# Layers 0 and 1 of a four-layer graph network: one sum of adjacency quarters by a raw load and an accumulating DMA in place of VectorE, and a list of nodes by the eight largest keys

## The chip, the core and the metric

The kernel runs on one core of one Trainium2 chip. The core has five engines with instruction streams of their own: TensorE (PE, with its weight load PEld), VectorE (DVE), ScalarE (ACT), GpSimd (POOL) and SyncE (SP); 16 DMA engines move data between HBM and SBUF. Plain loads and stores are here issued by SP, a few by ACT; POOL issues stores, indirect transfers and the DMAs that add to their destination. The metric is the device time of one execution in microseconds (us).

## The reference, cut to what matters

Sixteen graphs (batches) of 1024 nodes with 256 features go through four layers, each a pre-normed residual layer on the same adjacency matrix:

```python
h = jnp.maximum(_layernorm(x, axis=-1), 0.0)
x = x + _L0_gnn_ref(h, adj, ...)   # attention: a = adj*exp(e_i+f_j), rows scaled to sum 1; a @ (h W^T + b)
h = jnp.maximum(_layernorm(x, axis=-1), 0.0)
x = x + _L1_gnn_ref(h, adj, ...)   # d^-1/2 adj d^-1/2 @ (h W) + bias
h = jnp.maximum(_layernorm(x, axis=-1), 0.0)
x = x + _L2_gnn_ref(h, adj, ...)   # a recurrence over the nodes, one after the other
h = jnp.maximum(_layernorm(x, axis=-1), 0.0)
x = x + _L3_gnn_ref(h, adj, ...)   # adj @ h, a two-layer MLP with an RMS norm and silu
```

Layers 0 and 1 need, for every batch, the product of the 1024x1024 adjacency with a 1024x256 matrix twice (once per layer), and sums of its rows. Layer 2 walks through the nodes in order; the kernel groups nodes of each block of 128 that do not depend on each other, so it needs, beforehand, an order of the nodes computed from `adj`.

## The kernel before, in words

**Seven products instead of eight.** Each 1024x1024 product is cut into 2x2 blocks and done by Strassen's method in Winograd's form. The adjacency's four blocks of 512x512, each a tile of 128x4x512 fp32 (1 MB), are `b11`, `b21`, `b22` and one that is only used inside `t3`; four sums of blocks are `t1`, `t2 = t1 + b22`, `t3`, and `t4 = t2 + b21`. All live in ten buffers `at0` to `at9`, which the list `quarters` hands out and takes back in turn. `get` loads a block by SP. `plus(b, name, other)` adds one tile to another in place by a DMA that POOL issues (`accum_op=ADD`); it makes `t1` and `t3` of every batch but the first. `add_halves` makes a sum by two VectorE additions of 128x1024 each; it makes `t2` and `t4`. `keep` stores the four sums to HBM for layer 3. `drop` returns a buffer after the last product that reads it.

**`layers_0_1`** writes the order of all five engines out by hand (a manual schedule): instructions run on each engine in the order in which the code records them. A loop over i from 0 to 15 holds, for batch i, the sums of layer 0 (hooks `a0` to `a6`), the weights of layer 0, two pieces of the weights of layer 1 for batch i-1, the sums of layer 1 (hooks `d0` to `d6`), and the row sums (`degrees`) of batch i+1. `sums` (L387) does seven products of eight fp32 matmul passes each, in the order b11, b21, t2, t1, t3, t4 ("22"), b22, and calls one hook after each: so VectorE's and ScalarE's work for the loads, norms and sums of the next batch is laid between the products. VectorE combines the products' results in L397, L407, L411 and L414, and adds the weights' result to x in L427. `weights` (L423) multiplies by the 256x256 weight.

**Names that the change and the steps touch.** `a1` computes two combinations of h (`second`) and then `t4`. `get(i+1, "b11")` and the others fetch the next batch. In the last part of iteration i, `plus(i+1, "t3", "b22")`, the two `keep`s of `t1` and `t2`, one `plus_row` (POOL adds a bias row to a part of x, L362) and the taking of a buffer for `t4` follow each other. Further `plus_row`s stand in `a2_`, `a3`, `a4`. `Moments.first` and `Moments.second` let ScalarE sum and square x of the next batch for its norm (L337, L345); `normed` (L358) scales and cuts h. `inv_sqrt` computes roots on POOL (L86: `rs`, `dis`).

**Jobs.** From i = 9 to 15 two jobs per iteration, `run_a` and `run_b`, prepare layer 2 for two batches: they load `ad`, `ab`, `h2`; `mask` and `scale` (POOL, L524 to L532) change `ad`; `turn` and `order` transpose on PE and copy out by ScalarE and VectorE (L545, L572, L574); POOL stores `heT_d`, `near_d`, `next_d` and `base_d`. All need the node order.

**The order of the nodes.** `orders` is a generator of VectorE work on 128 rows (8 blocks of 16 batches), 128 nodes each. `places` gives each node a bin and a position (`pos`); `rest` then makes the list `node` (which node sits at position p), the index tables, and a chain over the nodes (L205, L206), fetching tiles `pc` by ACT's queue (L105) on the way. Each `yield` states a cost. `side(us)` in the hooks runs the generator until 1.25 times the given budget is used up: this is how the list's work is spread over the loop.

Of the kernel before, what the change touches and what calls it, by code (L numbers as in the profile page):

```python
# [11 lines left out]
ALU = mybir.AluOpType  # L12
# [4 lines left out]
P = 128  # L17
# [19 lines left out]
def bcast_row(ap, n):  # L37

    return bass.AP(tensor=ap.tensor, offset=ap.offset, ap=[[0, P], [1, n]])
# [3 lines left out]
def gnn_stack(ctx: ExitStack, tc: tile.TileContext, a: dict, out: bass.AP):  # L43
    nc = tc.nc
# [23 lines left out]
    step = const.tile([P, P], F32, name="step")  # L68
# [27 lines left out]
    def orders(pool, psum):  # L96
# [5 lines left out]
        def fetch(j0):  # L102
            def run():
                nz = pool.tile([P, R, P], F32, name="pc", bufs=3)
                nc.scalar.dma_start(nz, a["own"][:, j0 : j0 + R])  # L105
                pieces.append(nz)
            later.append(run)

        def piece(j0, op, value):
            nz = pieces.popleft()  # L110
            nc.vector.tensor_scalar(nz[:, :, j0:], nz[:, :, j0:], 0.0, value, op0=op, op1=ALU.mult)
            return nz

        def tile_(name, n=P):
            return pool.tile([P, n], F32, name="o_" + name)

        TOP = 1000.0
        bins, pos = tile_("bins"), tile_("pos")
        junk = tile_("junk")
        open_, below, held, fit = tile_("open", S), tile_("below", S), tile_("held", S), tile_("fit", S)  # L120

        def places():
            nc.vector.memset(bins, TOP)
            nc.vector.tensor_scalar(open_, step[:, :S], -1.0, TOP - 1, op0=ALU.mult, op1=ALU.add)
            nc.vector.tensor_scalar(below, open_, 1.0, None, op0=ALU.add)
            for k in range(S):
                nc.vector.memset(held[:, k : k + 1], -float(ALL_SLICES[k]) if k < NSL else 0.0)
            nc.vector.scalar_tensor_tensor(open_, held, 0.0, open_, op0=ALU.is_lt, op1=ALU.mult)
            for j0 in range(0, 3 * R, R):
                fetch(j0)  # L130
            yield 9.0
            for j0 in range(0, P, R):
                nz = piece(j0, ALU.is_equal, 2 * TOP)
                for j in range(j0, j0 + R):
                    mine = bins[:, j : j + 1]
                    nc.vector.scalar_tensor_tensor(fit, below, mine, open_, op0=ALU.is_le, op1=ALU.mult)
                    nc.vector.tensor_reduce(mine, fit, AX.X, ALU.max)
                    nc.vector.scalar_tensor_tensor(held, open_, mine, held, op0=ALU.is_equal, op1=ALU.add)
                    nc.vector.scalar_tensor_tensor(open_, held, 0.0, open_, op0=ALU.is_lt, op1=ALU.mult)
                    if j + 1 < P:  # L140
                        nc.vector.scalar_tensor_tensor(bins[:, j + 1 :], nz[:, j - j0, j + 1 :], mine, bins[:, j + 1 :],
                                                       op0=ALU.add, op1=ALU.min)
                    if j < j0 + R - 1:
                        yield 1.0
                if j0 + 3 * R < P:
                    fetch(j0 + 3 * R)
                yield 1.2

            key = tile_("key")
            nc.vector.scalar_tensor_tensor(key, bins, -256.0, step, op0=ALU.mult, op1=ALU.add)  # L150
            for i in range(0, P, R):
                less = pool.tile([P, R, P], F32, name="pc", bufs=3)
                nc.vector.tensor_tensor(less, key[:, None].to_broadcast([P, R, P]),
                                        key[:, i : i + R][:, :, None].to_broadcast([P, R, P]), ALU.is_lt)
                nc.vector.tensor_reduce(pos[:, i : i + R], less, AX.X, ALU.add)
                yield 1.4
            pt = psum.tile([P, 512], F32, name="pt")
            nc.tensor.transpose(pt[:, :P], pos, ident)
            nc.vector.tensor_copy(place, pt[:, :P])
            yield 0.5  # L160

        def rest():

            node = tile_("key")
            for p in range(P):
                nc.vector.scalar_tensor_tensor(junk, pos, float(p), step, op0=ALU.is_equal, op1=ALU.mult,
                                               accum_out=node[:, p : p + 1])
                if p % 4 == 3:
                    yield 1.6
            first = tile_("first", 2)  # L170
            nc.gpsimd.iota(first[:, :1], pattern=[[0, 1]], base=0, channel_multiplier=P, allow_small_or_imprecise_dtypes=True)
            of8 = tile_("of8", GB)
# [2 lines left out]
                                           accum_out=first[:, 1:])  # L175
# [25 lines left out]
            for j0 in range(0, P, R):  # L201
                nz = piece(j0, ALU.not_equal, 2.0)
                for j in range(j0, min(j0 + R, P - 1)):
# [3 lines left out]
                                                   op0=ALU.mult, op1=ALU.max)  # L207
# [56 lines left out]
    def layers_0_1():  # L264
        with ExitStack() as st:
# [7 lines left out]
            x, q, h1, h2, g, dis, mean, rs_of, ags = {}, {}, {}, {}, {}, {}, {}, {}, {}  # L273
# [14 lines left out]
            quarters = [big.tile([P, 4, 512], F32, name=f"at{k}") for k in range(10)]  # L288
            Q = {b: {} for b in range(B)}

            def get(b, name, m, n):
                Q[b][name] = quarters.pop(0)
                nc.sync.dma_start(Q[b][name], a["quarters"][b, m, n])

            def drop(b, name):
                quarters.append(Q[b][name])

            def keep(b, name):
                nc.sync.dma_start(t_d[name][b], Q[b][name])

            def plus(b, name, other):
                nc.gpsimd.dma_start(out=Q[b][name], in_=Q[b][other], accum_op=ALU.add)
# [53 lines left out]
            def normed(h, x, shift, scale, tiles):  # L356
                for t in tiles:
                    nc.scalar.activation(h[:, t], x[:, t], AF.Relu, bias=shift[:, t : t + 1], scale=scale[:, t : t + 1])  # L358
# [237 lines left out]
            def side(us):  # L596
                while later:
                    later.popleft()()
                left[0] += us * 1.25
                while left[0] > 0:  # L600
                    cost = next(math, None)
                    if cost is None:
                        break
                    left[0] -= cost
                left[0] = min(left[0], 0.0)

            all_ = range(NT)
            lo, hi = range(NT // 2), range(NT // 2, NT)
# [16 lines left out]
            def add_halves(b, to, left, right):  # L625
                for k in range(2):
                    nc.vector.tensor_add(half(Q[b][to], k), half(Q[b][left], k), half(Q[b][right], k))
# [5 lines left out]
            left_of, first, second = combos(q[0])  # L633
            first()
            add_halves(0, "t3", "t3", "b22")
            Q[0]["t4"] = quarters.pop(0)
            nc.sync.dma_start(vec["bias"], bcast_row(a["bias"], D))
            nc.sync.dma_start(w1, a["weight"].rearrange("(c p) e -> p c e", p=P))
            load_x(1)
# [6 lines left out]
            for i in range(B):  # L646
                run_a, run_b = jobs.get(i, (None, None))
                here, ahead, behind = i < B, i + 1 < B, i > 0
# [8 lines left out]
                def a1():  # L657
                    if ahead:
                        get(i + 1, "b11", 0, 0)
                    second()  # L660
                    add_halves(i, "t4", "t2", "b21")
                def a2_():
                    if ahead:
                        get(i + 1, "t1", 0, 1)
# [24 lines left out]
                def a5():  # L689
                    inverse(i, got["deg"])  # L690
                    if run_a:
                        run_a.scale()
                    if ahead:
                        mean[i + 1].first(hi)
                    side(1.8)
                def a6():
                    if ahead:
                        mean[i + 1].middle()
                        mean[i + 1].second(lo)
                    side(2.0)  # L700
                if here:
                    ag = sums(i, left_of, [a0, a1, a2_, a3, a4, a5, a6])
                    h1[i] = big.tile([P, NT, D], F32, name="h1")
                    m1 = Moments(x[i], "n", h1[i][:, 0])
                    weights(x[i], ag, w0, got["rc"], m1)
                    m1.root()
                    if ahead:
                        mean[i + 1].second(hi)

                def second_weights(pairs):  # L710
# [7 lines left out]
                if here:  # L718
                    rd = small.tile([P, NT], F32, name="rd")
                    nc.vector.tensor_mul(rd, m1.rs, dis[i])  # L720
                    shift = small.tile([P, NT], F32, name="shift")
                    nc.vector.tensor_mul(shift, m1.neg, rd)
                    normed(h1[i], x[i], shift, rd, all_)
                    if ahead:
                        mean[i + 1].root()
                second_weights(pairs)
# [64 lines left out]
                if ahead:  # L791
                    ds = degrees(i + 1)
                    plus(i + 1, "t3", "b22")
                    keep(i + 1, "t1")
                    keep(i + 1, "t2")
                    plus_row(x[i + 1], "W_b", 0)
                    Q[i + 1]["t4"] = quarters.pop(0)
                def late_norm():
                    h2[i - 1] = big.tile([P, NT, D], F32, name="h2", bufs=2)
                    normed(h2[i - 1], x[i - 1], m2.shift, m2.rs, all_)  # L800
# [1007 lines left out]
```

## Time and profile before

Three runs took 4202.88 us in the median (4201.75 to 4206.0). The profiled execution took 4201.68 us; its span, from the first to the last instruction, is 4199.8 us.

| | |
|---|---|
| PE busy | 4008.7 us, 95% of the span |
| PEld busy | 2796.3 us, 67% |
| DVE busy | 2614.5 us, 62% |
| ACT busy | 1634.5 us, 39% |
| POOL busy | 1648.1 us, 39% |
| mean granted TensorE clock | 0.986 |
| layers 0 and 1 (0 to 1330 us): PE, DVE, ACT, POOL busy | 1238.3, 966.2, 705.8, 449.3 us |
| the same: mean DMA share, rate | 0.73, 245 GB/s |
| `add_halves` (L627), 128x1024 | 68 instructions, median 1220 ns |
| list of nodes (L166), 128x128 | 128 instructions, median 291 ns, and 128 reads of the accumulator, 81 ns |
| accumulating DMA `at<-at` (L302) | 30 issues of 1 MB by POOL, 912 ns each in the median, 7.0 us to landing |

A profile row names the line, the engine, the operation and the tiles written and read; "idle before" is the time that the engine stood still ahead of it, with what ended the wait. The granted clock is the share of TensorE's full speed that the throttle allowed. A query of windows gives busy time and DMA share of any stretch; the timeline gives single instructions in order of time. In this profile the first product of batch i starts at 22 us for i = 0, 376 for 5, 445 for 6, 650 for 9, 740 for 10, 833 for 11, 925 for 12, 1021 for 13, 1113 for 14 and 1212 for 15.

### The profile page before, as it was taken

The numbers are of one execution on the slowest core, as the hardware profiler recorded it, in microseconds if no ns is written. First come the engines' busy times: TensorE is split into PE (matmuls) and PEld (weight loads), VectorE is DVE, ScalarE is ACT, GpSimd is POOL, SyncE is SP. The second block draws the span as 40 slices with busy tenths as digits, with TensorE's granted clock in tenths as the row PEclk, the third lists the DMA queues.
The fourth block names the chain that finished last, engine by engine and source line by source line (L and its number), as shares of the span: only waits on it lengthen the run. The fifth ranks groups of instructions, "written<-read, shape, count | busy, mean of one in ns | idle before, by whom it ended". The sixth has DMA issues, their size and how long they took to land. (4 is left out here: it accounts for less than half of the span.)

```text
span 4199.8 us, 56656 instructions
## 1 busy us (share of the span) xinstructions
PE 4008.7 (95%) x19307; PEld 2796.3 (67%) x19307; DVE 2614.5 (62%) x6218; ACT 1634.5 (39%) x4172; POOL 1648.1 (39%) x1740
## 2 busy tenths in 40 slices
PE   7999999999997999999999999998899999999998
PEld 3545455555554888888888888877465665656656
DVE  7888976477762434444444444454677877777776
ACT  3565655545543332322322232333333344333332
POOL 2232223434334324243333333332555364463552
PEclk9999999999999999999999999998999999999999
DMA  7576757988768454646454545431634434334320
GB/s 243 207 237 230 227 201 261 264 297 292 281 211 266 134 185 156 192 132 201 136 187 154 192 144 184 141 124 40 234 113 141 151 121 159 123 130 171 111 100 21
DMA packets 406702, 744.72 MB, mean 177 GB/s; under 512 B 75168, under 2 KB 325664, under 8 KB 365344
## 3 DMA queue, kind: packets, MB, share of 16 engines
q1 hardware_dynamic: 370976, 613.49, 42.6%
q0 software_dynamic: 26080, 109.21, 9.2%
q10 hardware_dynamic: 9216, 16.78, 1.1%
q8 instruction: 209, 3.42, 0.3%
q14 instruction: 221, 1.81, 0.1%
HBM read 538.85 MB, written 183.76 MB: 172 GB/s over the span
## 5 line engine op out<-in xcount | busy, mean ns | idle before, releaser
L86 POOL TENSOR_TENSOR rs<-rs_v,mhalf 128x8 f32<-128x8 f32 (+1 forms) x65 | 112.4, 1729 | 892.4 <-DVE rs_v L82 461.4
L935 PE MATMUL pf<-hb,ab 128*128 128x256 f32 x1568 | 415.2, 383 | 0.0
L1049 PE MATMUL pf<-hs,wx 128*128 128x256 f32 x1536 | 347.8, 382 | 14.5 <-POOL hs L1039 14.2
L1049 PEld LDWEIGHTS pf<-hs,wx 128*128 128x128 f32 x1536 | 291.7, 192 | 56.7 <-POOL hs L1039 15.3
L1592 POOL TENSOR_TENSOR ss<-ss,sq 128x512 f32<-128x512 f32 x224 | 299.6, 1353 | 22.9 <-ACT sq L1590 16.7
L1362 POOL DMA_INDIRECT hs_d<-h,table x128 | 129.3, 1010 | 444.4 <-ACT gates L1057 366.4
L935 PEld LDWEIGHTS pf<-hb,ab 128*128 128x128 f32 x1568 | 272.1, 191 | 37.3 <-issue 6.7
L1054 DVE TENSOR_TENSOR gates<-pf,bias 128x512 f32<-128x512 f32 x128 | 88.5, 692 | 283.5 <-PE pf L1049 249.2
L423 PE MATMUL pmm<-w,ag 128*128 128x256 f32 x1024 | 236.6, 390 | 17.0 <-DVE ag L414 7.6
L1655 PEld LDWEIGHTS po<-w,hh 128*128 128x128 f32 x2048 | 238.3, 193 | 16.6 <-issue 11.0
L1655 PE MATMUL po<-w,hh 128*128 128x128 f32 x2048 | 242.5, 277 | 1.4 <-ACT hh L1638 0.7
L423 PEld LDWEIGHTS pmm<-w,ag 128*128 128x128 f32 x1024 | 198.1, 195 | 57.8 <-DVE x L427 9.9
L1590 ACT ACTIVATE sq<-hh 128x512 f32<-128x512 f32 x224 | 141.6, 632 | 199.7 <-POOL ss L1592 123.0
L1538 PE MATMUL ph<-bxt,hb 128*128 128x512 f32 x440 | 200.7, 602 | 13.1 <-ACT hb L1510 10.5
L1147 ACT ACTIVATE r<-pr 128x128 f32<-128x128 f32 (+2 forms) x256 | 57.9, 278 | 353.4 <-PE pr L1103 293.5
L1085 PE MATMUL pf<-bd,h 128*128 128x384 f32 (+4 forms) x512 | 182.9, 449 | 1.4 <-DVE bxt L1088 1.4
L1088 DVE TENSOR_TENSOR bxt<-bxt,pf 128x384 f32<-128x384 f32 (+4 forms) x256 | 127.7, 501 | 82.1 <-PE pf L1085 79.7
L1588 DVE SCALAR_TENSOR_TENSOR hh<-ph,b,u 128x512 f32<-128x512 f32 x192 | 141.1, 749 | 43.9 <-PE ph L1584 34.1
L1638 ACT ACTIVATE hh<-hh,rw 128x512 f32<-128x512 f32 x256 | 158.9, 711 | 23.8 <-DVE hh L1637 23.8
L1538 PEld LDWEIGHTS ph<-bxt,hb 128*128 128x128 f32 x440 | 82.9, 193 | 111.3 <-issue 92.8
L345 ACT ACTIVATE pt<-x,m_neg 128x256 f32<-128x256 f32 x240 | 114.5, 477 | 107.7 <-DVE m_neg L340 101.3
L1637 DVE TENSOR_TENSOR hh<-hh,po 128x512 f32<-128x512 f32 x256 | 154.3, 679 | 2.9 <-PE po L1634 2.9
(371 smaller groups left out, 9246.8 us busy)
## 6 DMA issues: line engine op xcount, KB each, us to landing
at<-in_quarters SPq DMA_DIRECT2D x94, 1024.0 KB
t_d<-at SPq DMA_DIRECT2D x64, 1024.0 KB
ab<-in_columns SPq DMA_DIRECT2D x127, 512.0 KB
bxt<-t_d SPq DMA_DIRECT2D x42, 1024.0 KB
bxt<-in_quarters SPq DMA_DIRECT2D x34, 1024.0 KB
at<-at POOLq DMA_DIRECT2D x30, 1024.0 KB, 7.0
at<-t_d SPq DMA_DIRECT2D x22, 1024.0 KB
pc<-in_own ACTq DMA_DIRECT2D x64, 256.0 KB
```

Of the source, the lines that this page charges most:

```text
L423: nc.tensor.matmul(po[:, t - t0], ag[:, c, t * P : (t + 1) * P], w[:, c], start=c == 0, stop=c == DC - 1)
L935: nc.tensor.matmul(pb, ab[:, jts[k]], hb[:, jts[k]], start=k == 0, stop=k == len(jts) - 1)
L1049: nc.tensor.matmul(pg[:, e], wx[:, c, q * D + e * P : q * D + (e + 1) * P], self.hs[:, c], start=c == 0, stop=c == DC - 1)
L1085: nc.tensor.matmul(pf, h[:, g, c * P : (c + 1) * P], bd[:, g, b0 : b0 + n, S : S + far], start=True, stop=True)
L1362: nc.gpsimd.indirect_dma_start(out=hs_d[t][g][:, :], out_offset=row(1, g, t, s), in_=h[:, g], in_offset=None)
L1538: nc.tensor.matmul(pa, st[left][:, k], at[q % 6][:, k], start=onto is None and k == 0, stop=k == 3, skip_group_check=True)
L1588: behind3[:] = [nc.vector.scalar_tensor_tensor(hh[q][:, k], ph, b1[:, k : k + 1], u, op0=ALU.add, op1=ALU.add)]
L1590: nc.scalar.activation(sq, hh[q][:, k], AF.Square)
L1592: nc.gpsimd.tensor_tensor(ss[q], ss[q], sq, ALU.add)
L1637: nc.vector.tensor_mul(hh[q][:, k], hh[q][:, k], pr)
L1638: nc.scalar.activation(hh[q][:, k], hh[q][:, k], AF.Silu, scale=rw[:, k : k + 1])
L1655: nc.tensor.matmul(po[:, n], left[:, c, n * P : (n + 1) * P], right[:, c], start=onto is None and n == 0 and c == 0, stop=c == HH - 1, ski ...
```

## The change

1. `t4` is no longer added up by VectorE. A new function `raw_t4` takes the buffer and loads block (1, 0), which is what `b21` holds, into it a second time by SP; in `a1`, `plus(i, "t4", "t2")` adds `t2` to it by an accumulating DMA that POOL issues. The loads stand where the buffer was taken before: behind the `keep`s of `t1` and `t2`.
2. The list of nodes is no longer found position by position. The keys (bin and node in one number) are turned around so that the first node has the largest key; 16 times, `max` takes the eight largest of each row and `match_replace` sets them to 0. Five elementwise instructions and the one that turns the keys give the node's number from the key. The yields of this part sum to 12.8 units instead of 51.2.
3. In iterations with jobs, the budgets of `side` in `a5` and `a6` fall from 1.8 and 2.0 to 0.8 and 0.0.
4. In iterations with jobs, `mean[i + 1].second(hi)` (ScalarE) moves from behind the weights of layer 0 to behind `normed`, which stands after `run_a.turn`.

```diff
             nc.vector.scalar_tensor_tensor(key, bins, -256.0, step, op0=ALU.mult, op1=ALU.add)
+            nc.vector.tensor_scalar(bins, key, -1.0, 127.0, op0=ALU.mult, op1=ALU.add)
...
-            for p in range(P):
-                nc.vector.scalar_tensor_tensor(junk, pos, float(p), step, op0=ALU.is_equal, op1=ALU.mult,
-                                               accum_out=node[:, p : p + 1])
-                if p % 4 == 3:
-                    yield 1.6
+            for p in range(0, P, 8):
+                nc.vector.max(out=node[:, p : p + 8], in_=bins)
+                nc.vector.match_replace(out=bins, in_to_replace=node[:, p : p + 8], in_values=bins, imm_value=0.0)
+                yield 0.8
+            whole = 1.5 * 2.0 ** 31
+            nc.vector.tensor_scalar(junk, node, whole, None, op0=ALU.add)
+            nc.vector.tensor_scalar(junk, junk, whole, None, op0=ALU.subtract)
+            nc.vector.tensor_sub(node, junk, node)
+            nc.vector.tensor_scalar(node, node, 127.0, None, op0=ALU.add)
...
+            def raw_t4(b):
+                Q[b]["t4"] = quarters.pop(0)
+                nc.sync.dma_start(Q[b]["t4"], a["quarters"][b, 1, 0])
...
-            Q[0]["t4"] = quarters.pop(0)
+            raw_t4(0)
...
                     second()
-                    add_halves(i, "t4", "t2", "b21")
+                    plus(i, "t4", "t2")
...
-                    side(1.8)
+                    side(0.8 if run_a else 1.8)
...
-                    side(2.0)
+                    side(0.0 if run_a else 2.0)
...
-                    if ahead:
+                    if ahead and not run_a:
                         mean[i + 1].second(hi)
...
                     normed(h1[i], x[i], shift, rd, all_)
+                    if ahead and run_a:
+                        mean[i + 1].second(hi)
                     if ahead:
                         mean[i + 1].root()
...
-                    Q[i + 1]["t4"] = quarters.pop(0)
+                    raw_t4(i + 1)
```

## The prediction

> **What bounds the kernel now.** The page's busy table says TensorE (PE) 95%, VectorE (DVE) 62% of a 4199.8 us span. Its chain of waits covers only the last third, so it says nothing of layers 0 and 1, where every edit lies. I therefore read the table of windows (layers 0 and 1 end near 1330 us; PE is busy 1238.3 of those 1330 us), then the waits of PE there, in the two halves of the loop over batches. Columns: waiting op, what released it, total us, times, longest. First i = 1 to 8 (60 to 680 us), then i = 9 to 14 (680 to 1210 us), where the jobs `run_a` and `run_b` are added:
>
> ```profile
> PE pmm L423 <- DVE x L427: 4.5, 4, 1.4
> PE pz L387 <- DVE ag L407: 3.2, 6, 0.8
> ```
>
> ```profile
> PE pt L542 <- ACT pt L345: 8.1, 6, 2.2
> PE pmm L423 <- DVE ag L414: 7.6, 4, 3.5
> PE pt L565 <- ACT hT L572: 7.4, 6, 3.2
> ...
> PE pmm L423 <- DVE ag L411: 2.8, 1, 2.8
> PE pz L387 <- DVE ag L407: 2.1, 3, 1.1
> PE pmm L423 <- DVE x L427: 1.9, 1, 1.9
> ```
>
> PE is the bound, and DVE costs time only where PE waits for it: 7.7 us in the first half, 14.4 us in the second. A wait has a second price. Around the 3.48 us wait at 1050.5 us of i = 13, the windows read (PE, PEld, DVE, ACT, POOL busy, then clock, DMA share, GB/s):
>
> ```profile
> 1047.00:1054.00 7.00, 3.52 (x18) 2.75 (x16) 6.72 (x17) 0.00 (x0) 4.09 (x4) 1.00 1.02 427
> 1054.00:1058.00 4.00, 4.00 (x11) 2.84 (x12) 3.75 (x19) 3.16 (x11) 0.00 (x0) 0.58 0.82 315
> ```
>
> After the gap the granted clock is 0.58: the next 32 weight matmuls (L423) take 8.96 us, against 7.07 us for 32 undisturbed ones at 1285.7. The same comparison gives 1.8 us in i = 11, 3.7 us in i = 12 (14.2 us for 48 against 10.5), 1.8 us in i = 14: 9.2 us with i = 13's 1.9.
>
> **The change, part by part.**
>
> *Sum t4 leaves VectorE.* Out: 2 adds of 128x1024 per batch, 32 in all; a pair takes 2.35 us where nothing disturbs it (387.5 us), so 37.6 us. They stood in `a1`, ahead of every DVE step of the first sums that PE then waits for (L407, L411, L414, L427).
>
> *Node list.* Out: 128 instructions that follow each other every 0.335 us (600 us), 43 us. In: 16 `max` and 16 `match_replace`, in no row of the trace; nearest are a 128x128 scalar_tensor_tensor (0.29 us) and a reduction of 128x128 (0.38 us). A pair costs 0.5 us if each is like these, 1.0 us if `match_replace` counts double; I take 0.65, so 10 us, plus 6 elementwise 128x128 steps at 0.28. Net 31 us of DVE out, in i = 7 to 9; PE waits for DVE there 0.99 us (680 us), so this alone is worth next to nothing, at either price. Its yields fall from 51.2 to 12.8 units, so what follows (tables, then the chain, L205) comes one batch earlier: chain in i = 10 to 14 instead of 11 to 15. The 2.9 us wait of L225 for L226 at 1210 us moves to i = 14, behind the product of t2, and I let it cost the same.
>
> *Budgets.* In i = 9 to 14 `a5` gives 0.8 instead of 1.8 and `a6` 0 instead of 2.0; times 1.25 that is 3.75 us less list work ahead of L414 and L427. With the adds, DVE arrives some 6 us earlier than now at the step for which PE waits 2.8 to 3.5 us. But POOL's scaling of `ad` (L531, L532, 3.6 us at 1047.6) runs beside two-input DVE steps that stretch under it (L490: 1.60 us, alone 0.17), so a rest stays.
>
> *second(hi) after normed.* 4 squares and 4 accumulator reads, 2.6 us of ScalarE, stood ahead of the four copies of `turn` (L545), for which PE waited 8.1 us in six batches. Behind `normed` ScalarE next waits 2.4 us for PE anyway (1073.8), and POOL, whose `rs` comes 3 us later, next waits 5.4 us for DVE (1077.6). Gain 7.5; late next are the copies themselves, 0.2 us each.
>
> *What t4 adds.* 16 loads of 1 MB on SP's queue, issued behind `keep` of t2, and 16 accumulating DMAs on POOL's queue. POOL now waits for load and t2; behind it stand three `plus_row` (3.9 us of POOL) and `dis`; behind those nothing is due before the weights. SP's `keep` of t4 waits for the landing. The load takes 1 MB / 430 GB/s = 2.4 us, the accumulation 7.0 us (median of `at<-at` to landing). PE needs t4 at the product "22". For i = 6, PE's rows:
>
> ```profile
> 444.52 3.70 PE L387 MATMUL px<-at,q 128*128 128x512 f32 x8
> ...
> 463.50 3.68 PE L387 MATMUL py<-at,q 128*128 128x512 f32 x8
> ```
>
> SP issues `keep` of t2 at 441.5, so the load lands near 449; POOL is free at 446. The accumulation of t3 has the queue until about 453 (451 now), then 7 us: 460, 3.5 us ahead of 463.5. In i = 13 POOL's near_d, next_d and base_d precede it (last issue 1023.4) and its queue drains by 1028; 7 us more: 1035, with PE at 1039.7. So no wait, but little to spare.
>
> Here **a rule speaks against the change**. The Trainium skill, "DMA: Bandwidth & Descriptors", section Queues, rings and completion order: each DMA engine takes turns between its queues, packet by packet. SP's loads are queued at the same moment, so an even share would make the 7 us 14: landing at 1042 in i = 13 (2.3 late) and 467 in i = 6 (3.5 late), over 6 and 9 batches some 45 us. The trace answers with the queue's share at 1026 to 1028 us, when SP had issued two loads of 1 MB:
>
> ```profile
> q0 software_dynamic: 152, 0.51, 95.2%
> q1 hardware_dynamic: 1, 0.00, 0.1%
> ```
>
> POOL's queue (q0) had nearly all of the engines and SP's (q1) nothing. I take the row; the rule makes the rival below. The price falls on SP's loads: 9.4 us later per batch. The engines idle 434 to 442 and 470 to 484 in i = 6's neighbourhood, 962 to 974 and 1058 to 1068 later on, so it fits. `ad` arrives near 1044 instead of 1037, POOL wants it at 1046.3.
>
> A second rule of the skill, "SBUF — State Buffer", section Who interferes with whom: GpSimd writing descriptors can be shut out for a whole VectorE instruction in a two-port mode. By the rule each issue could take one `tensor_scalar` more (L111, mean 0.57 us), 9 us of POOL in all. The rows of the 30 accumulating issues read 0.87 to 1.09 us, so 0.2 at most, 3 us. Either is hidden: POOL is free for 14 us before `dis`.
>
> **Sum**, against the profiled execution (span 4199.8, 4201.7 with what lies around it): ScalarE order -7.5; L411, L414, L407, L427, 14.4, and one wait of 1.0 that the profile leaves unexplained (939.5 us), of which -12; clock 9.2, of which -7; first half: the 4.5 and 1.3 of L407's 3.2 lie behind the adds (the rest is in the second sums), -5. New waits (chain a batch earlier, ScalarE held by fetches of `pc`, a late t4 here or there): +6. Total -25: 4176.7; the median shown (4202.9) is 1.2 above its profiled run, so 4178.
>
> **Rivals.** About 8.4 us (0.2%) is what a measurement of this kernel tells from no change.
> 1. *Late t4 (slower).* PE waits at "22" in every batch. For: slack of 3.5 us, DMA share about 0.9 in the second half before 9.4 us per batch are added, 11 us for the accumulation of t1 at 417 beside a store. Against: the q0 row. It cancels the gain at 25 / 16 = 1.6 us per batch; at the rule's 45 us the sum is 4223. Chance 0.16.
> 2. *DVE was not the limit.* The waits change their releaser (POOL's stalls, `pc` fetches: in i = 13 ScalarE's copy of px came only at 1040.6, released by L111) and only ScalarE's order pays: 4196. For: PE is busy 94 to 100% of each 50 us in i = 3 to 8. Chance 0.19.
> 3. *Everything goes*: 8.1 + 15.4 + 9.2 + 5.8 = 38.5 us, nothing new: 4164. Chance 0.15.
> My own case has 0.50. That the edits do not do what they say is excluded by the instruction order: the 32 adds are gone, the DMAs stand where described.
>
> Faster: 0.48 of mine, 0.15, 0.05 of rival 2 = 0.68; same: 0.11 + 0.02 + 0.02 = 0.15; slower 0.17 (rival 1, and rival 2 gone wrong). Range 4160 (case 3 with its 4 us of slack) to 4206, which leaves out most of rival 1.
>
> **What would show it.** PE's wait for ACT at `turn` gone from 8.1 to about 1; waits for L414 and its kin in i = 9 to 14 from 15 to 3 us, clock at 1.0 after them; DVE busy down about 69 us; no wait of PE at "22" for a DMA. A row of PE at the py product released by `at<-at`, some us in each batch, would make the prediction wrong.

## The result, and the profile after

The changed kernel takes 4195.7 us in the median of 13 runs (4190.0 to 4200.6), the kernel before 4206.0 us in as many runs beside it (4201.8 to 4208.6): ratio 0.9974, 95% interval [0.9967, 0.9981]. By the ratio that is 11 us faster, where 25 were forecast. The profiled executions say the same: 4190.65 us (span 4188.9) after 4201.68.

Where the 11 us came from, and where more was won and lost again, is seen from the start of each batch's first product (us from the span's start, by the timeline of PE):

| start of batch | 1 | 6 | 9 | 10 | 11 | 12 | 13 | 14 | 15 |
|---|---|---|---|---|---|---|---|---|---|
| before | 95.0 | 444.5 | 650.1 | 740.3 | 832.7 | 924.6 | 1020.8 | 1113.3 | 1211.8 |
| after | 94.8 | 437.3 | 643.0 | 740.4 | 830.4 | 923.6 | 1015.4 | 1103.6 | 1201.0 |
| lead of after | 0.2 | 7.2 | 7.1 | -0.1 | 2.3 | 1.0 | 5.4 | 9.7 | 10.8 |

The first half wins 7 us. Iteration 9 alone spends all of it, and the iterations with jobs, which were to bring most of the gain, end with a net 3.7 us more. The view by windows says how much of this is idle time of PE (length of the stretch, PE busy, PEld, DVE, ACT, POOL busy, clock, DMA share, GB/s). First batches 1 to 8 and 9 to 14 before, then the same after:

```profile
95.00:650.10 555.10, 544.60 (x1797) 286.87 (x1793) 473.16 (x1501) 326.23 (x960) 151.73 (x113) 1.00 0.66 223
650.10:1211.80 561.70, 518.09 (x1953) 300.74 (x1950) 375.67 (x949) 297.54 (x819) 234.23 (x197) 0.98 0.84 277
```

```profile
94.80:643.00 548.20, 542.99 (x1798) 287.50 (x1794) 438.43 (x1361) 325.97 (x960) 159.46 (x122) 1.00 0.81 256
643.00:1201.00 558.00, 516.06 (x1952) 299.84 (x1950) 355.21 (x894) 293.04 (x812) 231.76 (x197) 0.98 0.90 301
```

In the first half PE is idle 5.2 us instead of 10.5. In the second it is idle 41.9 us instead of 43.6: what was won there was paid again. So the question is what iterations 9 to 14 pay.

The waits of PE in the first half of the changed kernel (60 to 680 us; waiting op, releaser, total us, times, longest). Lines moved with the diff: L387 is now L396, L423 is L432, L427 is L436, L407 is L416.

```profile
...
PE pz L396 <- DVE ag L416: 1.2, 3, 0.5
PE pmm L432 <- DVE x L436: 0.7, 1, 0.7
PE py L396 <- DMA at<-at: 0.3, 1, 0.3
```

The waits of 3.2 and 4.5 us are down to 1.2 and 0.7, and the only wait of PE for the accumulated `t4` is 0.3 us: rival 1 is out. The same view from 680 to 1210 us (L414 is now L423, L542 is L551, L545 is L554, L565 is L574, L572 is L581, L225 and L226 are L230 and L231):

```profile
PE pt L574 <- ACT hT L581: 15.6, 11, 5.0
PE pt L230 <- DVE o_key L231: 6.5, 1, 6.5
PE pmm L432 <- DVE ag L423: 6.3, 3, 2.6
PE pt L551 <- ACT hT L554: 3.1, 12, 0.3
```

The 8.1 us at `turn` for the squares are gone, and the waits for L411 and L414 (10.4 us together) have become 6.3. But PE's wait in `order`, for ScalarE's copy of the turned adjacency, has doubled from 7.4 to 15.6 us, and the wait at the chain's transposes has grown from 2.9 to 6.5. The longest of the former, in the timeline of iteration 9 (start, duration, engine, instruction, idle time ahead of it and its releaser):

```profile
682.58 0.65 POOL L557 DMA_DIRECT2D heT_d<-hT  x1 [1.52 <-ACT hT L554]
...
694.13 0.59 ACT L581 COPY hT<-pt 128x512 f32<-128x512 f32 x1 [5.05 <-DMA heT_d<-hT]
...
694.77 0.47 PE L574 MATMUL pt<-to,ad 128*128 128x128 f32 x1 [4.98 <-ACT hT L581]
```

`order` writes its result `ao` into the same buffer `hT` whose contents POOL has just sent to `heT_d`. The copy (L581) may not write until that 1 MB store has read the buffer, and this store lands 11.5 us after its issue; PE, which has only two PSUM buffers to transpose into, stops. Behind the stop the TensorE clock is down as well (granted clock 0.50 from 694.7 to 697 us: the transposes took 0.42 to 0.47 us, where undisturbed ones take 0.27 to 0.30, and the next product 5.02 us instead of 3.60). Another 2.86 us of the same kind follow at 738.2, then 1.8 to 2.2 us in each of iterations 10 to 12 and 0.6 in 14.

Why the store lands late: the DMA queues while the second of these stores was under way (729.7 to 737.5 us; packets, MB, share of 16 engines), and in the last row its time to landing:

```profile
q1 hardware_dynamic: 262, 1.87, 56.7%
q0 software_dynamic: 172, 1.28, 45.9%
...
heT_d<-hT POOLq DMA_DIRECT2D x1, 1024.0 KB, 7.7
```

Over the whole stretch the two queues look as if they shared the engines evenly, but they took them one after the other. From 729.7 to 732.7 us SP's queue q1 has them all, with the stores of `t1` and `t2` and the new load of `t4`, which SP had issued from 718.9 to 726.2 us. POOL's q0 has them from 734 to 737.5 us:

```profile
q1 hardware_dynamic: 173, 1.27, 100.2%
```

```profile
q0 software_dynamic: 158, 1.16, 94.6%
q1 hardware_dynamic: 34, 0.15, 10.2%
```

The first store, issued at 682.6 us, waits longer still. From 684.6 to 688 us q1 has 97.7% and q0 moves one packet; only then do the two share (688.5 to 693 us):

```profile
q0 software_dynamic: 122, 0.99, 52.0%
q1 hardware_dynamic: 127, 0.91, 47.9%
```

What SP has issued by then are a load for the next batch (up to 682.3 us) and its stores of `t3` and `t4`. They are late themselves. The same rows of SP in the changed kernel, and in e7 (below), which has no DMAs for `t4` from batch 9 on but the same first half and the same list:

```profile
648.10 13.27 SPq L188 DMA_DIRECT2D order_d<-o_sub  x8
...
682.37 0.86 SPq L308 DMA_DIRECT2D t_d<-at  x2
```

```profile
648.17 5.38 SPq L188 DMA_DIRECT2D order_d<-o_sub  x8
...
674.65 0.86 SPq L308 DMA_DIRECT2D t_d<-at  x2
```

The list's eight stores hold SP for 13.27 us instead of 5.38 while the accumulation of `t4` is under way (issued at 648.9 us, landing after 11.0), so the two stores come 7.7 us later, just ahead of POOL's store at 682.6.

Over layers 0 and 1 the mean DMA share rose from 0.73 to 0.84, and the accumulations themselves land after 11.2 us in the median, not 7.0. (The 7.0 was the median of the five landings, of 30, that the profile before tells.)

### The profile page after: what moved, and what is told of

Same layout as the page of the kernel before. It is cut to its first block, busy times and chain, and to the rows that moved or that the text cites. A ratio compares the mean times of both kernels' runs of the same rounds, so it can differ in the third digit from the quotient of the medians.

```text
span 4188.9 us, 56510 instructions
## 1 busy us (share of the span) xinstructions
PE 4007.3 (96%) x19307; PEld 2800.6 (67%) x19307; DVE 2546.6 (61%) x5983; ACT 1632.7 (39%) x4172; POOL 1659.4 (40%) x1756
## 5 line engine op out<-in xcount | busy, mean ns | idle before, releaser
L432 PE MATMUL pmm<-w,ag 128*128 128x256 f32 x1024 | 226.3, 380 | 7.0 <-DVE ag L423 6.3
L432 PEld LDWEIGHTS pmm<-w,ag 128*128 128x128 f32 x1024 | 193.5, 190 | 42.2 <-issue 8.1
L1549 PE MATMUL ph<-bxt,hb 128*128 128x512 f32 x440 | 200.2, 601 | 14.2 <-ACT hb L1521 11.2
L1549 PEld LDWEIGHTS ph<-bxt,hb 128*128 128x128 f32 x440 | 82.7, 193 | 112.2 <-issue 92.5
L1521 ACT ACTIVATE hb<-x,shift,rs 128x256 f32<-128x256 f32 x120 | 60.6, 588 | 233.7 <-DVE shift L1518 233.7
## 6 DMA issues: line engine op xcount, KB each, us to landing
at<-in_quarters SPq DMA_DIRECT2D x110, 1024.0 KB, 11.4
t_d<-at SPq DMA_DIRECT2D x64, 1024.0 KB, 10.0
at<-at POOLq DMA_DIRECT2D x46, 1024.0 KB, 11.2
bxt<-t_d SPq DMA_DIRECT2D x42, 1024.0 KB, 4.8
bxt<-in_quarters SPq DMA_DIRECT2D x34, 1024.0 KB, 5.0
at<-t_d SPq DMA_DIRECT2D x22, 1024.0 KB, 5.2
```

The source lines that it names most:

```text
L432: nc.tensor.matmul(po[:, t - t0], ag[:, c, t * P : (t + 1) * P], w[:, c], start=c == 0, stop=c == DC - 1)
L1549: nc.tensor.matmul(pa, st[left][:, k], at[q % 6][:, k], start=onto is None and k == 0, stop=k == 3, skip_group_check=True)
```

## Experiments

All times are medians of several runs, and ratios are against runs of the kernel before, made beside them on the same chip, with 95% intervals; a difference of two ratios is turned into us by 4206. "hT wait" is PE's wait for ScalarE's copy in `order` from 680 to 1210 us; "chain wait" that for VectorE at the chain's transposes, wherever they fall (e10: for ScalarE).

| kernel | t4 | list, yields | budgets and ScalarE order | `ao` in | us | ratio | hT wait | chain wait |
|---|---|---|---|---|---|---|---|---|
| before | VectorE | old, 51.2 | old | hT | 4206 to 4210 | 1 | 7.4 | 2.9 |
| after | DMA | new, 12.8 | new | hT | 4195.7 | 0.9974 [0.9967, 0.9981] | 15.6 | 6.5 |
| e1 | DMA | old, 51.2 | old | hT | 4217.8 | 1.0023 [1.0012, 1.0035] | 15.6 | 1.8 |
| e2 | VectorE | new, 12.8 | old | hT | 4196.0 | 0.9976 [0.9965, 0.9986] | 1.7 | 7.9 |
| e13 | VectorE | old, 51.2 | order only | hT | 4196.9 | 0.9981 [0.9972, 0.9990] | 9.0 | 2.9 |
| e14 | VectorE | old, 51.2 | budgets only | hT | 4194.3 | 0.9972 [0.9960, 0.9983] | 5.0 | 0.3 |
| e3 | VectorE | old, 51.2 | both | hT | 4186.6 | 0.9951 [0.9938, 0.9965] | 8.3 | 0.3 |
| e4 | DMA | new, 51.2 | both | hT | 4197.8 | 0.9986 [0.9978, 0.9993] | 22.8 | 0.3 |
| e5 | VectorE | new, 12.8 | both | hT | 4194.7 | 0.9970 [0.9958, 0.9982] | 1.6 | 8.8 |
| e8 | load only | new, 12.8 | both | hT | 4202.3 | 0.9987 [0.9980, 0.9994] | 11.9 | 8.8 |
| e7 | DMA to batch 8 | new, 12.8 | both | hT | 4186.7 | 0.9952 [0.9939, 0.9966] | 1.8 | 8.8 |
| e6 | DMA | new, 12.8 | both | dead tiles | 4181.5 | 0.9940 [0.9926, 0.9953] | 1.4 | 6.5 |
| e10 | DMA | new, 12.8 and 6.0 | both | dead tiles | 4178.7 | 0.9928 [0.9914, 0.9941] | 1.4 | 0.6 |
| e9 | DMA | new, 51.2 | both | dead tiles | 4177.4 | 0.9924 [0.9911, 0.9938] | 1.4 | 0.2 |
| e12 | VectorE | new, 51.2 | both | dead tiles | 4180.0 | 0.9929 [0.9915, 0.9942] | 1.3 | 0 |
| e11 | VectorE | old, 51.2 | both | dead tiles | 4174.7 | 0.9919 [0.9906, 0.9933] | 1.3 | 0 |
| e15 | DMA to batch 8 | old, 51.2 | both | dead tiles | 4171.4 | 0.9918 [0.9905, 0.9932] | 1.3 | 0 |

### One part at a time

The first theory was that the list's phase took the gain back: its transfers of 4-byte elements now stand in iterations 8 and 9, its transposes in iteration 14. The rival was the DMA traffic of `t4`.

**e1**, only `t4` changes hands (`raw_t4` is as in the change):

```diff
-                    add_halves(i, "t4", "t2", "b21")
+                    plus(i, "t4", "t2")
...
-                    Q[i + 1]["t4"] = quarters.pop(0)
+                    raw_t4(i + 1)
```

> Only t4's sum changes hands (load plus accumulating DMA); list of nodes, budgets and ScalarE's order are those of before. If the missing gain went to the list's phase (its DMAs of 4-byte elements in i = 8 and 9, its transposes in i = 14): the first half keeps its 7 us, the second wins some 5 more at the waits for L414 and L427, ScalarE's 8 us stay: 4190 to 4196. If it went to t4's own DMA traffic, which delays the stores of heT_d: 7 us won, 7 lost, 4200 to 4206.

It is slower than before: 4217.8 us, beyond what either theory said. Its waits from 680 to 1210 us, in the view used above (L569 is `order`, L546 `turn`):

```profile
PE pt L569 <- ACT hT L576: 15.6, 5, 4.4
PE pt L546 <- ACT pt L349: 9.4, 6, 2.2
```

By the timeline batch 9 begins 5.9 us earlier than before, and batch 15 11.5 us later. The list stands where it stood, so the doubled wait for the copy in `order` belongs to `t4`'s traffic.

**e2**, only the list with its shorter yields (the part of the diff from `max` to the last `tensor_scalar`):

> Only the list of nodes by eight largest keys, with its shorter yields. By the list's phase: slower than before by 5 to 10 us (4208 to 4213), with a wait of several us for heT_d in i = 9 although t4 is summed as before. By t4's traffic: no wait at heT_d over 1 us, and 4200 to 4206.

Both times were wrong: it is 10 us faster. The wait for the store that the list's phase would have made is not there (1.7 us in all). Iteration 13 does lose 6.9 us (99.4 against 92.5), with 7.14 us of wait at the transposes. But the chain ends in that iteration, and iteration 14 falls from 98.5 to 86.4 us: the waits for L414 (2.8) and at the transposes (2.9), seen there before, have no counterpart. So what the list is worth seems to depend on which iteration its last steps fall in, not on its 31 us of VectorE; e12 and e11 below agree, where the new list with the old yields wins nothing over the old list.

**e3**, budgets and ScalarE's order alone, then each by itself:

```diff
-                    side(1.8)
+                    side(0.8 if run_a else 1.8)
...
-                    if ahead:
+                    if ahead and not run_a:
                         mean[i + 1].second(hi)
...
+                    if ahead and run_a:
+                        mean[i + 1].second(hi)
```

> Only the budgets of a5 and a6 and the squares of hi behind normed. By the prediction's terms: 7.5 us of ScalarE's order and at most 4 of 14 us at L411, L414, L427: 4191 to 4196, by either theory. If the squares behind normed hold up the copies of order (L572): 4200 or more.

> The kernel before with the squares of hi behind normed, and nothing else. By the prediction's term: PE's 8.1 us of waits at turn go and 7.5 us are won, 4197 to 4201. If the waits go and come back at the copies of order (L572, for the store of heT_d): PE's waits there rise from 7.4 to 12 or more, 4203 or more.

> The kernel before with the two smaller budgets in i = 9 to 14, and nothing else. By the prediction's terms, in which a large part of the 14.4 us at L411, L414, L407 and L427 needs t4's adds out of VectorE's way too: 2 to 5 us won, 4202 to 4205. If the budgets alone do it (the 20 us of both edits together less ScalarE's 7.5): 10 to 13 us won, 4194 to 4198.

Both edits together give 0.49%, 21 us, twice the change as a whole. The order alone gives 0.19% (8.0 us), the budgets alone 0.28% (11.8 us), and the two add up. e13's first waits from 680 to 1210 us:

```profile
PE pt L565 <- ACT hT L572: 9.0, 11, 3.7
PE pmm L423 <- DVE ag L414: 7.1, 4, 3.0
```

The wait of L542 for the squares (8.1 us) is gone, and the wait in `order` has taken over 1.6 us of it. In e14 the waits for L414 (7.6 us) and L427 (1.9) are gone from this stretch, but those for L411 rise from 2.8 to 8.9 and those for L407 from 2.1 to 3.9: VectorE's four waits are 12.8 us together, before 14.4. The starts of the batches show the gain in iterations 10 and 11 (87.4 and 87.1 us against 92.4 and 91.9) and in 14 (93.3 against 98.5). The windows from batch 9 to the start of batch 15, e13 first, then e14:

```profile
651.40:1207.10 555.70, 514.38 (x1951) 298.46 (x1949) 373.76 (x949) 296.97 (x819) 233.98 (x198) 0.99 0.85 280
651.40:1202.40 551.00, 513.80 (x1936) 300.46 (x1933) 351.36 (x865) 293.28 (x812) 229.89 (x192) 0.98 0.84 278
```

PE's 43.6 us of idle time fall to 41.3 in e13 and to 37.2 in e14, by 2.3 and 6.4 us. Of the 8.1 us at `turn`, most came back as other waits; faster matmuls bring the rest. In e14 what fell beside VectorE's 1.6 us are waits for which no edit was made (7.4 to 5.0 us in `order`, 2.9 to 0.3 at the chain's transposes). Why the smaller budgets do this was not shown.

### Phase or traffic

**e4** is the changed kernel with the list's total yield restored, so that tables and chain fall about where they fell before:

```diff
-                yield 0.8
+                yield 3.2
```

> The changed kernel, but every pair of max and match_replace yields 3.2 instead of 0.8, so that tables and chain fall where they fell in before. By the list's phase: the 4.98 us wait of i = 9 for heT_d and the 6.5 us one in i = 14 go, 10 us faster than the changed kernel (4183 to 4188). By t4's traffic: within 3 us of the changed kernel, with the waits for heT_d still there.

The transposes fall in iteration 15 and PE waits 0.3 us there. But the hT wait is 22.8 us and the time is no better (4197.8). **e5** takes only `t4`'s DMAs out of the changed kernel:

```diff
-                    plus(i, "t4", "t2")
+                    add_halves(i, "t4", "t2", "b21")
...
-                    raw_t4(i + 1)
+                    Q[i + 1]["t4"] = quarters.pop(0)
```

> The changed kernel with t4 summed by VectorE again (list, budgets and ScalarE's order stay). If t4's DMA traffic is what took the gain back (copies of order waiting for the store of heT_d): 15 to 25 us faster than the changed kernel, 4172 to 4182, with waits of PE for hT of order at 8 us or less. If the shorter list and not the traffic matters: within 4 us of the changed kernel.

The hT wait falls to 1.6 us as the traffic theory says, but the time is that of the changed kernel. The first waits of e5 from 680 to 1210 us show what stands in its place:

```profile
PE pt L230 <- DVE o_key L231: 8.8, 1, 8.8
PE pmm L428 <- DVE ag L419: 8.1, 4, 2.7
PE pz L392 <- DVE ag L412: 5.8, 4, 1.8
```

VectorE is the limit again, at the transposes above all. So there are two losses, one with `t4`'s DMAs, one with the list in its new place: e3, with neither, is 0.35% faster than e4, 0.19% (8 us) faster than e5 and 0.23% faster than the changed kernel. The intervals of e3 and e5 overlap at their ends, those of e3 and the other two lie apart.

**e8** keeps SP's load of `t4`, but VectorE's adds write over it:

```diff
-                    plus(i, "t4", "t2")
+                    add_halves(i, "t4", "t2", "b21")
```

> The changed kernel with the raw load of t4 kept, but the sum made by VectorE over it (the load's data are overwritten): SP's load alone, with no accumulating DMA. If the load, which stands beside the store of heT_d and moves SP's queue, makes the waits for hT of order: they stay at 10 us or more and the time is 4190 to 4200. If the accumulation on POOL's queue makes them: 8 us or less, and the time that of the kernel without t4's DMAs plus at most 4 us.

The time to landing of stores to `heT_d` (least, median, most) in e5 and in e8. Of 16 stores each profile tells it for three, the same in both, `run_b`'s in iterations 10, 12 and 14:

```profile
DMA to landing us min/median/max: 4.4/4.4/4.6
```

```profile
DMA to landing us min/median/max: 6.1/6.4/6.9
```

The load alone makes these stores 2.0 us later, about the 2.4 us that the prediction worked out for 1 MB, and the hT wait 11.9 us; it costs 0.17% (7 us) against e5. Putting the accumulating DMA in place of the adds then wins 0.13% (5.5 us) back: on balance `t4`'s DMAs bring nothing in the changed kernel.

**e6** leaves all DMAs as they are and takes the dependence away. `run_a`'s result goes into a buffer of `ag`, `run_b`'s into that of `h1`, whose contents nobody needs at that time, so the copies no longer wait for the store (no more SBUF is used):

```diff
-            jobs[15][1].names = {"ao": "h1"}
+            for run_a, run_b in jobs.values():
+                run_a.names = {"ao": "ag"}
+                run_b.names = {"ao": "h1"}
```

(A further line lets `ao` use the two buffers of `ag`.)

> The changed kernel in full, but order's result goes to the buffer of a dead tile (ag for run_a, h1 for run_b) instead of hT's, so that its copies need not wait until the store of heT_d has read hT. By the traffic theory: PE's waits of 15.6 us for them fall to 2 or less, with the slow matmuls after them 15 to 20 us are won: 4176 to 4182. If the waits only change their name (the stores of near_d and next_d, or the loads behind them): 4190 or more.

4181.5 us, 0.34% (14 us) less than the changed kernel, as the theory says, though stores still land late (4.3, 5.4 and 10.3 us for the three that the profile tells). Its waits from 680 to 1210 us:

```profile
PE pt L230 <- DVE o_key L231: 6.5, 1, 6.5
PE pmm L432 <- DVE ag L423: 6.1, 4, 2.3
PE pt L475 <- DMA at<-in_quarters: 5.2, 1, 5.2
...
PE pt L574 <- ACT ag L581: 1.4, 6, 0.2
```

15.6 us have become 1.4. A part comes back as 5.2 us of waiting for a load of the next batch. The 14 us are not the price of `t4`'s traffic alone: e11 below makes the same edit on e3, without that traffic, and wins 0.32% (13 us).

**e7** uses the DMAs for `t4` in batches 0 to 8 alone:

```diff
-                    plus(i, "t4", "t2")
+                    if i <= 8:
+                        plus(i, "t4", "t2")
+                    else:
+                        add_halves(i, "t4", "t2", "b21")
```

> The changed kernel with t4 by load and accumulating DMA in batches 0 to 8 alone, where no heT_d is stored, and by VectorE from batch 9 on. By the traffic theory this keeps the 7 us of the first half and has none of the losses of the second: 5 to 8 us faster than the kernel without t4's DMAs, 4165 to 4175. By the rival, in which the first half's gain comes from the list and is there without t4: equal to the kernel without t4's DMAs.

It is 0.18% (7.6 us) faster than e5, as forecast for the difference; the absolute figure was missed, since e5's was. Batch 9 begins at 643.0 us as in the changed kernel (e5: 653.3). The comparison that isolates the loss is the one with the changed kernel, from which e7 differs in `t4`'s DMAs of batches 9 to 15 alone: without them it is 0.22% (9 us) faster, the intervals lie apart, and the hT wait is 1.8 us instead of 15.6, although VectorE makes these sums again.

### Putting it together

With `ao` in dead tiles: **e9** adds the yields of e4; **e10** instead puts one `yield 6.0` ahead of the chain's transposes; **e12** is e9 with `t4` on VectorE; **e11** has neither `t4`'s DMAs nor the new list; **e15** is e11 with `t4`'s DMAs in batches 0 to 8.

> The changed kernel in full, order's result in the buffers of dead tiles, and the list's yields 3.2 (tables and chain where before had them). If the two losses are separate (22.8 us of waits for hT with the list in its old place, 6.5 us at the transposes of the chain with it in its new place), both are gone: 4168 to 4175, the fastest of all. If they hide one another: 4179 to 4185, as with the buffers alone.

> The changed kernel in full with order's result in dead tiles, and a yield of 6.0 ahead of the chain's transposes, which then fall one to three products later in i = 14. If PE waits there because VectorE still has the chain's last steps ahead of it: the wait of 6.5 us falls below 3, 4174 to 4179. If the wait is VectorE's lateness of the whole batch: it stays at 5 or more or moves to the next L423, 4180 to 4184.

> The kernel before with the budgets, ScalarE's order and order's result in dead tiles: neither t4's DMAs nor the new list. Against the same without the buffers (0.9951) the 8.3 us of waits for hT go: 4174 to 4180. If t4's DMAs and the new list are worth anything once nothing waits for heT_d, this is 5 us or more slower than the version with both and the list in its old place; if not, it is as fast or faster.

> As the version with dead tiles and the list's yields at 3.2, but with t4 summed by VectorE. If t4's DMAs gain once nothing waits for heT_d (7 us in the first half): 5 to 9 us slower than that version, 4174 to 4182. If their traffic still costs what it gains: within 3 us of it.

> The kernel before with budgets, ScalarE's order, order's result in dead tiles, and t4 by load and accumulating DMA in batches 0 to 8 alone. If the first half's gain of t4's DMAs is kept where no job shares the DMA engines: 5 to 8 us faster than the same without t4's DMAs (0.9919), 0.990 to 0.991. If it is lost later, when the batches come earlier but the list does not: 0.9915 or more.

All five lie between 0.9918 and 0.9929 with overlapping intervals. The transposes' wait of 6.5 us falls to 0.6 by the one yield, but the time by only 0.12%, inside the intervals. e9 was to be at most 4175; its first wait says why it is not:

```profile
PE pt L475 <- DMA at<-in_quarters: 6.0, 1, 6.0
```

In e12, without `t4`'s DMAs, this wait is 1.2 us, yet e12 is as fast within the intervals: the traffic delays another transfer now, while without it VectorE keeps PE waiting 9.3 us at L428 for L416 (e9: 4.0). e15 has its 6.7 us of lead over e11 at batch 9 (644.7 against 651.4), still has 6.7 at batch 14, and then loses 6.2 in iteration 14, where PE waits 5.0 us once for VectorE's L415. What makes VectorE late there in e15 and not in e11 was not followed further. So e11 and e15 have the lowest medians, 0.8% below the kernel before: the two small edits, with `ao` in dead tiles. Neither the new list nor `t4`'s DMAs add anything to them that can be measured.

## Why the prediction was right and wrong

**SP's loads 9.4 us later, "so it fits": this step failed.** It asked only whether the engines have idle gaps for 9.4 us more, and whether the loads' own readers could wait. It did not ask which other transfers of that time are waited for. The stores of `heT_d` are, because `order` reuses their buffer. The trace before had the sign of it, 7.4 us of PE waiting for L572, a number which the prediction quoted and gave no term. It became 15.6 us, and with `t4`'s DMAs kept out of batches 9 to 15 (e7) it is 1.8 us and the kernel 9 us faster.

**New waits, +6: mis-sized.** From e3 to the changed kernel, the list in its new place adds 8 us (e5) and `t4`'s DMAs in batches 9 to 15 add 9 (e7 against the changed kernel): 17, not 6. The wait of L225, moved at "the same cost", grew from 2.9 to 6.5 us. Two rows of VectorE and POOL in iteration 14 show a part of it:

```profile
1108.02 4.02 DVE L221 SCALAR_TENSOR_TENSOR o_junk<-o_sub,o_bins 128x128 f32<-128x128 f32 x1
```

```profile
1107.82 4.06 POOL L371 TENSOR_TENSOR x<-x,W_b_sb 128x512 f32<-128x512 f32 x3
```

The chain's last steps stand in one row ahead of the transposes, and one of them, which takes 0.29 us in the median, lasts as long as POOL's three `plus_row`s beside it.

**`t4` in time: right, by a row read wrongly.** PE never waits more than 0.3 us for it. But the accumulation takes 11.2 us, not 7.0. The Trainium skill, page "DMA: Bandwidth & Descriptors", section "Queues, rings and completion order", says that an engine takes turns between its queues. The prediction set this aside for a row of 2 us, 1026 to 1028, in which POOL's queue had 95.2% and SP's 0.1%. POOL had issued its stores there from 1021.5 to 1024.0 us, SP its loads from 1024.9 on. From 1028 to 1032 us it is the other way round: q1 95.5%, q0 3.5%. So the row shows the queue that came first, not one that goes ahead of the other, and at both stores shown above SP's came first. The rule agrees with the trace in one stretch, 688.5 to 693 us (52.0 and 47.9%); the 3.4 us before it and the 3 us from 729.7, in which one queue had all, it does not explain.

**ScalarE's order, -7.5: the size right, in part by luck.** Alone it gives 8.0 us (interval 4 to 12), and the 8.1 us are gone from `turn`, where the copies' own waits stay (3.1 us, before 2.9). But PE's idle time falls by 2.3 us only; the rest is faster matmuls, for which the sum had a term of its own.

**First half, -5: right, a little small.** PE's idle time there falls by 5.3 us; 7.1 us are won in the trace, 7.6 by e7 against e5. (The prediction's view of it left out two rows, 6.1 us for L358 and 3.0 for L155; both are still there.)

**VectorE's waits in iterations 9 to 14, -12: mis-sized.** The four waits fall from 14.4 to 7.3 us in the changed kernel (L423 and L416). Neither edit does it alone: they are 13.8 us in e1, which only takes the adds away, and 12.8 in e14. That the budgets alone win 11.8 us (7 to 17) has thus another cause than this term, and it stays open.

**Clock, -7: right only where it was looked for.** The 32 weight matmuls behind the gaps at 865.6, 956.7 and 1047.4 us take 7.2 us each, not 8.9. But the clock falls behind the new waits instead, and from batch 9 to the start of batch 15 PE's busy time falls by 2.0 us in all, its mean clock staying at 0.98.

**The sum, redone from runs that differ by one part each:** order and budgets -20.6 us (e3), the new list +8.0 (e5), `t4`'s DMAs in batches 0 to 8 -7.6 (e7), the same in batches 9 to 15 +9.3 (the changed kernel). These steps add up to the measured -11 by construction. By the intervals each is uncertain by 6 to 8 us, so the +8.0 and the -7.6 are barely clear of noise; for the -7.6 the traces speak as well, in which batch 9 begins 10.3 us earlier in e7 than in e5. The prediction's terms for order, VectorE's waits and the clock in iterations 9 to 14 were -26.5.

**The rivals.** Rival 2's time, 4196, is what came out, but in part by luck, for its mechanism is half right: the waits did change their releaser, though to a store and not to `pc` fetches, and the budgets paid as well as ScalarE's order. Rivals 1 and 3 are out. VectorE's busy time fell by 67.9 us (69 forecast; the list's elementwise steps are five in all, not six), and the pair of `max` and `match_replace` costs 0.66 us (0.65 taken):

```profile
L167 DVE MAX8 o_key<-o_bins x16: 285/294/296, 534.9 to 576.9; 128x8 f32<-128x128 f32 x16
...
L168 DVE MATCH_VALUE_LOAD o_bins<-o_key,o_bins x16: 92/92/93, 535.2 to 577.2; 128x8 f32 x16
L168 DVE MATCH_REPLACE8 o_bins<-o_key,o_bins x16: 274/275/278, 535.3 to 577.3; 128x128 f32<-128x128 f32 x16
```

POOL's issues of the accumulations did not lengthen beside VectorE (918 ns in the mean, 927 before).

**Still open:** single waits of 1.0 to 3.3 us for "issue" at the fifth product of layer 0 (the one with `t3`), in iterations 11 and 12 of most kernels here, have no releaser in the profile; how much of e2's and e5's differences is due to the list's tables, its chain or its transposes was not told apart; why the smaller budgets win 12 us is not shown, nor why a queue whose DMA is issued second moves nothing for 3 to 5 us.

## What to carry to other kernels

Before adding DMA traffic, list the transfers of that time whose end releases something, stores whose buffer is written again above all, and see what each would have to wait behind: here a store issued behind another queue's transfers moved nothing for 3 to 5 us. A wait for such a store that already shows in the profile is where the cost will land. Split a view of queues over several us before reading it as sharing. Try the parts of a change one by one: here two small edits alone were worth twice the whole, and the two large ones, added to them, took half of that back. A dead tile as the target of a copy won 13 to 14 us, more than the work taken from VectorE.

## What the runs showed that was not expected

Tiny packets fill the DMA engines. Of the stretch from 678 to 698 us in the changed kernel (40 slices: busy tenths of the DMA engines, then GB/s) the first 4.5 us are nearly full while 1 to 41 GB/s move; a table of the list is loaded then, and 7061 of the 8577 packets of the whole stretch are under 512 bytes:

```profile
DMA  9999998109907799987999999989989999999979
GB/s 26 41 25 9 8 7 4 1 1 115 131 0 246 311 393 262 262 229 262 360 426 393 442 426 426 459 360 492 442 360 475 393 399 393 350 385 383 383 262 356
```

The length of a gap alone does not say whether the clock falls behind it: 32 weight matmuls took 7.17 us behind a wait of 2.55 us in the changed kernel, and 8.86 us behind one of 2.33 us in e6.
